# Spectral filter layer: 32 filter rows become 16, split by token parity over two halves of the rows, with summed and differenced output matrices

## Chip, cores and metric

The kernel runs on one core of a Trainium2 chip. The metric is the device time in microseconds (us) of one launch; before the change the median of three runs is 7736.49 us (7729.43 to 7759.1). The engines are named as the profile names them: PE is TensorE (PEld its weight loads), DVE is VectorE, ACT is ScalarE, POOL is GpSimd, SP is SyncE, whose queue issues nearly all DMAs here.

## What is computed

A network of four layers works on x of 64 images, each 11 x 11 = 121 tokens of 128 channels, in float32. Each layer adds a state-space mixer and then a feed-forward part to x. Only the feed-forward part of the last layer (index 3), a spectral transform unit, is changed. Cut to what matters:

```python
# phi: 16 filters in time; sgn(t) = +1 for even t, -1 for odd t
U_plus[t, k]  = sum_{s<=t} phi[k, t-s] * u[s]                    # per image and channel
U_minus[t, k] = sgn(t) * sum_{s<=t} phi[k, t-s] * sgn(s) * u[s]
out  = sum_k sigma[k]**0.25 * (U_plus[:, k] @ Mpp[k] + U_minus[:, k] @ Mpm[k])
out += sum_{i<3} shift(u, i) @ Mu[i]
# four such results for the first T, T//2, T//4, T//8 tokens, each with its own M,
# mixed by the weights softmax(log_weights + gumbel) in straight-through form
x = x + mix(layernorm(x))
```

The tokens fall into four bands: 0 to 14, 15 to 29, 30 to 59 and 60 to 120. A band gets contributions from as many of the four results as reach it; the last band has only the first.

## The kernel before, in words

Tokens lie on the partitions: `X` is a view of `HX`, 121 rows (D) by 64 images by 128 channels. The state-space mixer uses the same memory for its scan, and at its end loads X from DRAM in groups of eight images (L878, and L880 for the last group, which is stored last). After the feed-forward part, X is stored in groups of eight (L1432).

`stu_layer` (L1226) is emitted in program order, and a scheduler of the language then orders each engine's instructions by priority (program order) and readiness in its own model of time, so that a later instruction can go ahead of one that isn't ready. It handles the waits between engines. The parts are:

- Set-up. `stu_filters` forms the filters for the three early bands. `ahead` (L1254) holds the 16 filters as Toeplitz matrices; a matmul with the reversed identity `turned` (L1259) puts its rows in token order, and ScalarE copies the columns of the last band into `filt` (L1260). `filt` is scaled by sigma (L1266). A second set of 16 rows is made from the first with the signs of token and column (L1271), for U_minus. `M` (L1275), 32 matrices of 128 x 128, comes by one DMA; `MU` is the three shift matrices.
- `turned_in(b0)` (L1298) normalises eight images into `u`, and puts their transposes, with channels on the partitions, into `uT`.
- `last_band(b0, u)` (L1321) makes the last band for eight images. For each eight of the 32 filter rows, eight matmuls `pu` (L1327), one an image, have the image's tokens and channels as weights and 8 filters x 61 columns as moving data; VectorE and ScalarE copy the results in turn (`leave`, L1290) into `U`. Then eight matmuls `acc` (L1330) multiply `U` with the matrices and add up in one PSUM tile. Three more (L1332) add the shifts. The sum goes to `oT`.
- `matrices(i)` (L1308) folds a seventh of the filter matrices for the early bands: it loads a piece `m` (L1314), multiplies (L1316), copies to `ka` and stores it to `KD` in DRAM (L1319). The loop at L1348 goes over the first seven groups of images: `turned_in` of the next, `last_band` of this one, `matrices`.
- Then come the early bands in the order 2, 1, 0 (L1354): matmuls of all images against matrices read back from `KD` (L1370), summed in the PSUM tile `out` of four banks, which one buffer serves for all three bands; copies to `oT` (L1380).
- `turned_out` (L1337) transposes `oT` back, eight images at a time, and VectorE adds it to X. The last group's `last_band` and `turned_out` come at the very end.

PSUM has eight banks: three buffers for `mm` tiles (`pu`, `pt`, `pa`, `px`), one for `acc`, four for `out`. In the mixture-of-experts layer of layer 0, `moe_layer`, the matmul `px<-oe,P` (L1061) takes 64 rows of tokens' experts, at row 0 for one half and row 64 for the other.

Of the kernel before, what the change touches and what calls it, by code (L numbers as in the profile page):

```python
# [8 lines left out]
F32 = mybir.dt.float32  # L9
BF16 = mybir.dt.bfloat16  # L10
AF = mybir.ActivationFunctionType
ALU = mybir.AluOpType
AX = mybir.AxisListType
PSUM = bass.MemoryType.PSUM
DRAM = bass.MemoryType.DRAM

D = 121
C = 128
L = 256
NS = 16  # L20
E = 64
BANDS = ((0, 15), (15, 30), (30, 60), (60, 121))


class Ctx:
# [12 lines left out]
        nc.vector.memset(self.eps5, 1e-5)  # L38


def bcast(ap, n):

    return ap.unsqueeze(2).to_broadcast([ap.shape[0], ap.shape[1], n])


def layer_norm(cx, pool, dst, src, eps):

    nc = cx.nc
    G = src.shape[1]
    st = pool.tile([D, G, 6], F32, name="ln_st")  # L50
    mv = pool.tile([D, G, 2], F32, name="ln_mv")
    r = pool.tile([D, 2, G], F32, name="ln_r")
    for i in range(G):
        nc.vector.bn_stats(st[:, i, :], src[:, i, :])
    for i in range(G):
        nc.vector.bn_aggr(mv[:, i, :], st[:, i, :])

    nc.scalar.activation(r[:, 0, :], mv[:, :, 1], AF.Ln, bias=eps[:D])
    nc.scalar.activation(r[:, 0, :], r[:, 0, :], AF.Exp, scale=-0.5)
    nc.vector.scalar_tensor_tensor(r[:, 1, :], mv[:, :, 0], -1.0, r[:, 0, :], ALU.mult, ALU.mult)  # L60

    def apply():
        for i in range(G):
            nc.scalar.activation(
                dst[:, i, :], src[:, i, :], AF.Identity, bias=r[:, 1, i : i + 1], scale=r[:, 0, i : i + 1]
            )

    return apply
# [11 lines left out]
CB = 8  # L80
# [18 lines left out]
class Conv:  # L99
# [679 lines left out]
    def run(self):  # L779
        NC, G = self.NC, 2 * self.NC * PAIRS  # L780
# [92 lines left out]
        assert not self.plan and not early and not self.pre  # L873
        ahead()
        load(1)
        X = self.cx.X
        for c in range(NC - 1):
            self.nc.sync.dma_start(X[:, CB * c : CB * c + CB, :], self.dst(CB * c, CB))  # L878
        finish()
        self.nc.sync.dma_start(X[:, CB * NC - CB :, :], self.dst(CB * NC - CB, CB))  # L880


def conv_part(cx, v):
# [342 lines left out]
def stu_layer(cx, l, load):  # L1226
# [1 line left out]

    tc, nc, a, X, NB = cx.tc, cx.nc, cx.a, cx.X, cx.NB
    ident = cx.ident
    p = f"L{l}_ffn_"
    GB = 8
    CC = 2400
    T3 = BANDS[3][0]
    N3 = D - T3
    with ExitStack() as ctx:
        enter = ctx.enter_context
        keep = enter(tc.tile_pool(name=f"sk{l}", bufs=1))  # L1240
        work = enter(tc.tile_pool(name=f"sx{l}", bufs=2))
        ps = enter(tc.tile_pool(name=f"sp{l}", bufs=3, space=PSUM))
        ps_a = enter(tc.tile_pool(name=f"sa{l}", bufs=1, space=PSUM))

        sw = stu_filters(cx, l, keep)


        filt = keep.tile([D, 32, N3], F32, name="filt")
        phi = a[p + "phi"]
        nf, span = phi.shape  # L1250


        ahead = work.tile([D, 16, D], F32, name="ahead", tag="U")
        nc.sync.dma_start(ahead, bass.AP(tensor=phi.tensor, offset=phi.offset, ap=[[1, D], [span, nf], [1, D]]))  # L1254
        turned = keep.tile([D, D], F32, name="turned")
        nc.vector.tensor_copy(turned, ident[:D, D - 1 :: -1])
        for f in range(0, 16, 8):
            pf = ps.tile([D, 8, N3], F32, name="pf", tag="mm")
            nc.tensor.matmul(pf, turned, ahead[:, f : f + 8, T3:], start=True, stop=True)  # L1259
            nc.scalar.copy(filt[:, f : f + 8, :], pf)  # L1260
        sigma = keep.tile([D, 16], F32, name="sigma")
        nc.sync.dma_start(sigma, a[p + "sigma"].to_broadcast([D, 16]))
        nc.scalar.activation(sigma, sigma, AF.Sqrt)
        nc.scalar.activation(sigma, sigma, AF.Sqrt)
        nc.vector.tensor_scalar_mul(sigma, sigma, sw[:D, 0:1])
        nc.vector.tensor_mul(filt[:, 0:16, :], filt[:, 0:16, :], bcast(sigma, N3))  # L1266

        sgn = keep.tile([D, 2], F32, name="sgn")
        nc.sync.dma_start(sgn, a["sgn"])
        for odd in range(2):  # L1270
            nc.vector.tensor_scalar_mul(filt[:, 16:32, odd:N3:2], filt[:, 0:16, odd:N3:2], sgn[:, odd : odd + 1])  # L1271


        M = keep.tile([C, 32, C], F32, name="M")
        nc.sync.dma_start(M, a[p + "M"][:32].rearrange("k (d e) -> d k e", e=C))  # L1275
        MU = keep.tile([C, 4, 3, C], F32, name="MU")
        for i in range(4):
            z = 3 - i
# [5 lines left out]

        load()
        uT = keep.tile([C, NB, D], F32, name="uT")
        oT = keep.tile([C, NB, D], F32, name="oT")
        turn = 0

        def leave(dst, src):  # L1290
            nonlocal turn
            turn += 1
            if turn % 2:
                nc.vector.tensor_copy(dst, src)  # L1294
            else:
                nc.scalar.copy(dst, src)  # L1296

        def turned_in(b0):  # L1298
            u = work.tile([D, GB, C], F32, name="u", bufs=3)
            layer_norm(cx, work, u, X[:, b0 : b0 + GB, :], cx.eps5)()  # L1300
            for b in range(0, GB, 4):
                pt = ps.tile([C, 4, D], F32, name="pt", tag="mm")
                for i in range(4):
                    nc.tensor.transpose(pt[:, i, :], u[:, b + i, :], ident[:D, :D])
                leave(uT[:, b0 + b : b0 + b + 4, :], pt)
            return u

        def matrices(i):  # L1308

# [10 lines left out]

        def last_band(b0, u):  # L1321
            acc = ps_a.tile([C, GB, N3], F32, name="acc")
            for f0 in range(0, 32, 8):
                U = work.tile([C, 8, GB, N3], F32, name="U")
                for b in range(GB):
                    pu = ps.tile([C, 8, N3], F32, name="pu", tag="mm")
                    nc.tensor.matmul(pu, u[:, b, :], filt[:, f0 : f0 + 8, :], start=True, stop=True)  # L1327
                    leave(U[:, :, b, :], pu)
                for f in range(8):
                    nc.tensor.matmul(acc, M[:, f0 + f, :], U[:, f], start=(f0 + f == 0), stop=False)  # L1330
            for j in range(3):
                nc.tensor.matmul(  # L1332
                    acc, MU[:, 3, j, :], uT[:, b0 : b0 + GB, T3 - j : D - j], start=False, stop=(j == 2)
                )
            leave(oT[:, b0 : b0 + GB, T3:], acc)

        def turned_out(b0):  # L1337
            for b in range(b0, b0 + GB, 4):
                px = ps.tile([D, 4, C], F32, name="px", tag="mm")
                for i in range(4):  # L1340
                    nc.tensor.transpose(px[:, i, :], oT[:, b + i, :], ident)
                xs = X[:, b : b + 4, :]
                nc.vector.tensor_add(xs, xs, px)
# [10 lines left out]
        for z in (2, 1, 0):  # L1354
            t0, t1 = BANDS[z]
            n = t1 - t0
            per = min(512 // n, NB)
            out = ps_a.tile([C, 4, 512], F32, name="out")
            for k0 in range(0, NZ[z], KL):
                kn = min(KL, NZ[z] - k0)  # L1360
                K = work.tile([C, KL, C], F32, name="K", bufs=3)
                r0 = R0[z] + k0
                nc.sync.dma_start(K[:, :kn, :], cx.KD[r0 : r0 + kn].rearrange("r (d e) -> d r e", e=C))
                if k0 == 0:
                    nc.vector.tensor_add(K[:, :3, :], K[:, :3, :], MU[:, z])
                for k in range(k0, k0 + kn):
                    s0 = max(t0, k)
                    for i in range(-(-NB // per)):
                        b0, bn = i * per, min(per, NB - i * per)
                        nc.tensor.matmul(  # L1370
                            out[:, i, : bn * n].rearrange("p (b t) -> p b t", t=n)[:, :, s0 - t0 :],
                            K[:, k - k0, :],
                            uT[:, b0 : b0 + bn, s0 - k : t1 - k],
                            start=(k == 0),
                            stop=(k == NZ[z] - 1),
                            skip_group_check=True,
                        )
            for i in range(-(-NB // per)):
                b0, bn = i * per, min(per, NB - i * per)
                leave(oT[:, b0 : b0 + bn, t0:t1], out[:, i, : bn * n].rearrange("p (b t) -> p b t", t=n))  # L1380
        for b0 in range(0, end, GB):
            turned_out(b0)
        last_band(end, u)
# [7 lines left out]
def metaformer_kernel(ctx: ExitStack, tc: tile.TileContext, a: dict, out: bass.AP):  # L1391
# [32 lines left out]
    for l in range(4):  # L1424
        conv_part(cx, v)
        kept.close()
        if l < 3:
            v, kept, passing, weights = mixer(l + 1)
        dst = outr if l == 3 else mid[2 * l + 1]
        FFN[l](cx, l, weights if l < 3 else lambda: None)  # L1430
        for b0 in range(0, NB, GB):
            nc.sync.dma_start(dst[:, b0 : b0 + GB, :], cx.X[:, b0 : b0 + GB, :])  # L1432
        if l < 3:
            passing.close()

# [59 lines left out]
```

## Time and profile before

| What | us |
|---|---|
| median of three runs | 7736.49 |
| the profiled execution's own time | 7752.68 |
| its span, first to last instruction | 7750.9 |
| the chain leaves the mixer (last load of X issued) | 6962 |
| PE's first matmul of the changed layer (L1259) | 6992.8 |
| first `pu` / first `acc` matmul | 6999.0 / 7006.4 |
| one pass of the loop over groups of images | 65.2 to 66.8 |
| early bands (L1370) | 7464.4 to 7677.9 |
| last group's `last_band` | 7686.8 to 7743 |

The mean granted TensorE clock is 0.85 over the span, and 0.95 to 0.97 in the loop's passes. The busy time of all engines over the span: PE 6041.0, DVE 5659.8, ACT 5449.4, POOL 5293.3 us.

How to read the lines. A group of instructions is given by line, engine, operation, `out<-in` by the program's names, shapes (for PE: rows*columns of the weights, then partitions x elements of the moving data) and count, then busy time and mean ns of one, then the engine's idle time just before them and what ended it. A stretch (A:B) gives for each engine its busy time and, in brackets, the number of instructions, then the granted PE clock, the share of time the DMA engines were busy and GB/s. The chain of waits follows the work that ended last back in time: start, us, what. A float32 matmul appears as two records. Matmuls are pipelined and their ends are modelled, so their starts say more than their lengths.

### The profile page before, as it was taken

How to read it: one execution, taken by the hardware profiler on the slowest of the kernel's cores; microseconds unless marked ns; L12 is line 12 of the kernel's file. 1: busy time of each engine (PE TensorE's matmuls, PEld its weight loads, DVE VectorE, ACT ScalarE, POOL GpSimd, SP SyncE). 2: the span in 40 equal slices, each digit the busy share in tenths (PEclk: the TensorE clock that was granted, in tenths of full speed). 3: DMA queues.
4: the chain of work that ended last, by engine and by line, in shares of the span. 5: the costliest groups of instructions: out<-in, count | busy, mean ns of one | idle time of the engine just before them, and what ended most of it. 6: DMA issues, size and time to landing. Idle time of an engine off the chain costs nothing. (4 is left out here: it accounts for less than half of the span.)

```text
span 7750.9 us, 208787 instructions
## 1 busy us (share of the span) xinstructions
PE 6041.0 (78%) x84334; PEld 3448.5 (44%) x84334; DVE 5659.8 (73%) x7849; ACT 5449.4 (70%) x12343; POOL 5293.3 (68%) x2659
## 2 busy tenths in 40 slices
PE   6788778776788877766788888767678887758999
PEld 3444444465344444444344444434344444434445
DVE  5888888844788888962788888871788888872201
ACT  7888888733888888853788888862788888852200
POOL 6798999812888888931888888940888898960000
PEclk8888898777898989875889989875788888879999
DMA  7899999856899999942899999951899999971111
GB/s 181 227 247 243 245 246 243 215 167 170 221 241 249 246 240 244 247 110 75 220 241 244 246 248 243 243 140 37 217 236 243 243 245 241 245 184 46 35 39 36
DMA packets 905471, 1536.54 MB, mean 198 GB/s; under 512 B 136840, under 2 KB 617442, under 8 KB 904503
## 3 DMA queue, kind: packets, MB, share of 16 engines
q1 hardware_dynamic: 903223, 1521.09, 76.3%
q8 instruction: 662, 10.85, 0.6%
q14 instruction: 306, 2.51, 0.1%
q10 hardware_dynamic: 1280, 2.10, 0.1%
HBM read 1265.98 MB, written 256.97 MB: 196 GB/s over the span
## 5 line engine op out<-in xcount | busy, mean ns | idle before, releaser
L675 POOL TENSOR_TENSOR ub<-ub,Bt 128x1024 f32<-128x1024 f32 (+1 forms) x1984 | 4557.2, 2323 | 589.7 <-DMA ub<-uD 447.1
L699 ACT ACTIVATE da<-da,A 128x255 f32<-128x255 f32 x7744 | 3291.7, 451 | 696.1 <-PE da L686 612.0
L707 DVE TENSOR_TENSOR_SCAN H<-da,ub 128x512 f32<-128x512 f32 x2048 | 2391.8, 1208 | 354.4 <-POOL ub L675 183.9
L707 DVE TENSOR_TENSOR_SCAN HX<-da,ub 128x512 f32<-128x512 f32 (+1 forms) x1856 | 2130.4, 1190 | 318.5 <-POOL ub L675 160.1
L686 PE MATMUL da<-R,pick 120*128 120x255 bf16 x7744 | 1658.9, 305 | 546.0 <-DVE H L707 277.3
L686 PEld LDWEIGHTS <-pick 120*128 120x128 bf16 x7744 | 662.9, 103 | 1494.6 <-issue 1054.9
L728 PE MATMUL yb<-H,Cz 128*16 128x64 f32 x32768 | 782.2, 236 | 187.7 <-ACT yst L745 107.7
L728 PE MATMUL yb<-HX,Cz 128*16 128x64 f32 x32768 | 813.4, 237 | 122.6 <-DVE HX L707 62.7
L728 PEld LDWEIGHTS yb<-HX,Cz 128*16 128x16 f32 x32768 | 531.3, 105 | 641.9 <-issue 338.1
L728 PEld LDWEIGHTS yb<-H,Cz 128*16 128x16 f32 x32768 | 540.9, 103 | 584.0 <-issue 313.3
L263 PE MATMUL pc<-w_conv,xnT 128*121 128x256 f32 x1344 | 458.7, 433 | 27.4 <-ACT d L358 18.6
L184 POOL MEMSET t<- 128x2048 f32 x4 | 7.2, 1805 | 599.6 <-PE px L1221 211.8
L313 PE MATMUL pd<-t,w_dt 122*128 122x512 f32 x480 | 317.6, 749 | 101.7 <-ACT t L274 55.1
L745 ACT COPY yst<-yb 128x512 f32<-128x512 f32 (+2 forms) x640 | 334.9, 551 | 83.9 <-DMA yD<-yst 70.2
L743 DVE TENSOR_TENSOR yst<-yst,yb 128x512 f32<-128x512 f32 (+2 forms) x640 | 337.1, 543 | 73.7 <-PE yb L728 73.2
L340 PE MATMUL pr<-sp,ident 128*128 128x512 f32 x480 | 302.7, 717 | 80.0 <-ACT sp L301 75.0
L333 POOL TENSOR_TENSOR u<-sp,t 128x512 f32<-128x512 f32 x240 | 307.6, 1282 | 33.9 <-DMA uD<-u 32.8
L1294 DVE COPY U<-pu 128x488 f32<-128x488 f32 x128 | 85.4, 667 | 282.5 <-PE pu L1327 282.5
L1296 ACT COPY U<-pu 128x488 f32<-128x488 f32 x128 | 72.9, 570 | 308.7 <-PE pu L1327 308.7
L652 POOL TENSOR_TENSOR Cz<-Cp,own 128x512 f32<-128x512 f32 x256 | 275.5, 1076 | 0.0
L329 ACT CAST d<-sp 128x512 bf16<-128x512 f32 x240 | 148.6, 619 | 172.1 <-DMA dD<-d 171.9
L263 PEld LDWEIGHTS pc<-w_conv,xnT 128*121 128x121 f32 x1344 | 211.7, 194 | 94.9 <-ACT d L358 25.0
(237 smaller groups left out, 7243.8 us busy)
## 6 DMA issues: line engine op xcount, KB each, us to landing
ub<-uD SPq DMA_DIRECT2D x1920, 512.0 KB
dD<-d SPq DMA_DIRECT2D x256, 384.0 KB
R<-dD SPq DMA_DIRECT2D x192, 420.0 KB
uD<-u SPq DMA_DIRECT2D x256, 256.0 KB
yD<-yst SPq DMA_DIRECT2D x512, 60.5 KB
y<-yD SPq DMA_DIRECT2D x112, 242.0 KB
bcD<-bc SPq DMA_DIRECT2D x128, 128.0 KB
w1g<-in_L_ffn_weight_dram SPq DMA_DIRECT2D x16, 1024.0 KB
```

The costliest lines, as they stand in the source:

```text
L263: nc.tensor.matmul(pc, lhs, rhs, start=(j == 0), stop=(j == taps - 1))
L313: nc.tensor.matmul(s["p"], self.w_dt[:, k, :], tb[: D + 1], start=True, stop=True)
L333: nc.gpsimd.tensor_mul(s["u"], s["sp"], tb)
L340: nc.tensor.matmul(s["pr"], self.cx.ident, s["sp"], start=True, stop=False, skip_group_check=True)
L652: self.nc.gpsimd.tensor_mul(self.Cz[u], C.unsqueeze(2).to_broadcast([128, 64, CB]), self.own.unsqueeze(1).to_broadcast([128, 64, CB]),)
L675: self.nc.gpsimd.tensor_mul(x, x, self.bc[m, "Bt"].unsqueeze(1).to_broadcast([128, n, L]))
L686: self.nc.tensor.matmul(self.da[g % RING][:, j, 1:], self.pick[:n, d % 5].rearrange("p n b -> p (n b)"), self.R[m, d // 35][:n, d % 35 // ...
L699: self.nc.scalar.activation(x, x, AF.Exp, scale=self.A[:, m % 2, d : d + 1])
L707: self.nc.vector.tensor_tensor_scan(self.H[dq % 2][:, :n, p - DQ[dq][0]], self.da[g % RING].rearrange("p j l -> p (j l)")[:, :n], x.rearra ...
L728: self.nc.tensor.matmul(self.yb[32 * q : 32 * q + 16, slot % 8, :, :, :w], self.Cz[slot // 8][:, place % 64 : place % 64 + 2, :].rearrange ...
L743: nc.vector.tensor_add(dst, dst, src)
L745: nc.scalar.copy(dst, src)
```

## The change

In `stu_layer`, X, `u` and `filt` are laid out by token parity: even tokens in rows 0 to 60, odd tokens in rows 64 to 123 (`ROWS` is 124). With E and O the sums over even and odd tokens, U_plus is E + O, and U_minus is E - O at even output tokens and O - E at odd ones. So `pu` makes E and O with the same 16 filter rows, from the two halves of the rows, in matmuls of 61 or 60 rows and 4 filters x 61 columns, alternately on either half, and with two images to a PSUM tile. The matrices become Mpp + Mpm and Mpp - Mpm: E at even tokens and O at odd ones take the sum, the others the difference. `acc` is split by output parity into 31 and 30 columns for eight images. The columns of `filt` have even tokens first. The same `oT` gets its columns by parity, so that transposing it gives X's new rows. X is loaded and stored with one DMA for each parity in layer 3; layers 0 to 2 keep theirs. `mm` tiles get seven buffers, and `out` becomes tiles of that kind, one bank each; `U` becomes two tiles of 4 filters with four buffers in all; `ahead` takes a buffer of `u`.

```diff
+    def parted(self, b, n):
+        for rows, odd in ((slice(0, ODD - 3), 0), (slice(ODD, ROWS), 1)):
+            yield self.HX[rows, b * C : (b + n) * C].rearrange("p (b c) -> p b c", c=C), odd
+
+    def load_x(self, l, b, n, src):
...
+        for x, odd in self.parted(b, n):
+            self.nc.sync.dma_start(x, src[odd::2])
...
-        ps = enter(tc.tile_pool(name=f"sp{l}", bufs=3, space=PSUM))
+        ps = enter(tc.tile_pool(name=f"sp{l}", bufs=7, space=PSUM))
...
-        ahead = work.tile([D, 16, D], F32, name="ahead", tag="U")
+        ahead = work.tile([D, 16, D], F32, name="ahead", tag="u", bufs=3)
...
-        for odd in range(2):
-            nc.vector.tensor_scalar_mul(filt[:, 16:32, odd:N3:2], filt[:, 0:16, odd:N3:2], sgn[:, odd : odd + 1])
...
+        for k in range(0, 16, 8):
+            low = work.tile([C, 8, C], F32, name="low", tag="U", bufs=4)
+            nc.vector.tensor_sub(low, M[:, 0, k : k + 8], M[:, 1, k : k + 8])
+            nc.vector.tensor_add(M[:, 0, k : k + 8], M[:, 0, k : k + 8], M[:, 1, k : k + 8])
+            nc.scalar.copy(M[:, 1, k : k + 8], low)
...
+            pt = [ps.tile([C, GB, ODD - 3], F32, name="pt", tag="mm") for _ in range(2)]
+            for i in range(GB):
+                for odd, rows in enumerate((slice(0, ODD - 3), slice(ODD, ROWS))):
+                    n = rows.stop - rows.start
+                    nc.tensor.transpose(pt[odd][:, i, :n], u[rows, i, :], ident[rows, rows])
...
-            for f0 in range(0, 32, 8):
-                U = work.tile([C, 8, GB, N3], F32, name="U")
-                for b in range(GB):
-                    pu = ps.tile([C, 8, N3], F32, name="pu", tag="mm")
-                    nc.tensor.matmul(pu, u[:, b, :], filt[:, f0 : f0 + 8, :], start=True, stop=True)
-                    leave(U[:, :, b, :], pu)
-                for f in range(8):
-                    nc.tensor.matmul(acc, M[:, f0 + f, :], U[:, f], start=(f0 + f == 0), stop=False)
+            for f0 in range(0, 16, 4):
+                U = [work.tile([C, 4, GB, N3], F32, name="U", bufs=4) for _ in range(2)]
+                for b in range(0, GB, 2):
+                    pu = [ps.tile([C, 2, 4, N3], F32, name="pu", tag="mm") for _ in range(2)]
+                    for i in range(2):
+                        for s in range(2):
+                            rows = slice(ODD, ROWS) if s else slice(0, ODD - 3)
+                            nc.tensor.matmul(
+                                pu[s][:, i], u[rows, b + i, :], filt[rows, f0 : f0 + 4, :], start=True, stop=True
+                            )
+                    for s in range(2):
+                        leave(U[s][:, :, b : b + 2, :].rearrange("c f b t -> c b f t"), pu[s])
+                for f in range(4):
+                    for m in range(2):
+                        for odd, c0, c1 in halves:
+                            nc.tensor.matmul(
+                                acc[:, :, c0:c1],
+                                M[:, m, f0 + f, :],
+                                U[m ^ odd][:, f, :, c0:c1],
...
+            out_by_rows(b0, GB, T3, acc, True)
...
-            out = ps_a.tile([C, 4, 512], F32, name="out")
+            out = [ps.tile([C, 512], F32, name="out", tag="mm") for _ in range(-(-NB // per))]
```

More of the change, by code (lines that the diff above doesn't have):

```diff
@@ L22 @@
 BANDS = ((0, 15), (15, 30), (30, 60), (60, 121))
+ODD = 64
+ROWS = ODD + D // 2
 class Ctx:
@@ L38, in __init__, with store_x @@
         nc.vector.memset(self.eps5, 1e-5)
+    def parted(self, b, n):
+        for rows, odd in ((slice(0, ODD - 3), 0), (slice(ODD, ROWS), 1)):
+            yield self.HX[rows, b * C : (b + n) * C].rearrange("p (b c) -> p b c", c=C), odd
+    def load_x(self, l, b, n, src):
+        if l < 3:
+            self.nc.sync.dma_start(self.X[:, b : b + n, :], src)
+            return
+        for x, odd in self.parted(b, n):
+            self.nc.sync.dma_start(x, src[odd::2])
+    def store_x(self, l, b, n, dst):
+        if l < 3:
+            self.nc.sync.dma_start(dst, self.X[:, b : b + n, :])
+            return
+        for x, odd in self.parted(b, n):
+            self.nc.sync.dma_start(dst[odd::2], x)
 def bcast(ap, n):
@@ L49, in layer_norm @@
     G = src.shape[1]
-    st = pool.tile([D, G, 6], F32, name="ln_st")
-    mv = pool.tile([D, G, 2], F32, name="ln_mv")
-    r = pool.tile([D, 2, G], F32, name="ln_r")
+    n = src.shape[0]
+    st = pool.tile([n, G, 6], F32, name="ln_st")
+    mv = pool.tile([n, G, 2], F32, name="ln_mv")
+    r = pool.tile([n, 2, G], F32, name="ln_r")
     for i in range(G):
@@ L56, in layer_norm @@
         nc.vector.bn_aggr(mv[:, i, :], st[:, i, :])
-    nc.scalar.activation(r[:, 0, :], mv[:, :, 1], AF.Ln, bias=eps[:D])
+    nc.scalar.activation(r[:, 0, :], mv[:, :, 1], AF.Ln, bias=eps[:n])
     nc.scalar.activation(r[:, 0, :], r[:, 0, :], AF.Exp, scale=-0.5)
@@ L875, in run @@
         load(1)
-        X = self.cx.X
         for c in range(NC - 1):
-            self.nc.sync.dma_start(X[:, CB * c : CB * c + CB, :], self.dst(CB * c, CB))
+            self.cx.load_x(self.l, CB * c, CB, self.dst(CB * c, CB))
         finish()
-        self.nc.sync.dma_start(X[:, CB * NC - CB :, :], self.dst(CB * NC - CB, CB))
+        self.cx.load_x(self.l, CB * NC - CB, CB, self.dst(CB * NC - CB, CB))
 def conv_part(cx, v):
@@ L1226, in stu_layer @@
 def stu_layer(cx, l, load):
-    tc, nc, a, X, NB = cx.tc, cx.nc, cx.a, cx.X, cx.NB
+    tc, nc, a, NB = cx.tc, cx.nc, cx.a, cx.NB
+    X = cx.HX[:ROWS].rearrange("p (b c) -> p b c", c=C)
     ident = cx.ident
@@ L1237, in stu_layer @@
     N3 = D - T3
+    NE = N3 - N3 // 2
+    halves = ((0, 0, NE), (1, NE, N3))
     with ExitStack() as ctx:
@@ L1241, in stu_layer @@
         work = enter(tc.tile_pool(name=f"sx{l}", bufs=2))
-        ps = enter(tc.tile_pool(name=f"sp{l}", bufs=3, space=PSUM))
+        ps = enter(tc.tile_pool(name=f"sp{l}", bufs=7, space=PSUM))
         ps_a = enter(tc.tile_pool(name=f"sa{l}", bufs=1, space=PSUM))
         sw = stu_filters(cx, l, keep)
-        filt = keep.tile([D, 32, N3], F32, name="filt")
+        filt = keep.tile([ROWS, 16, N3], F32, name="filt")
         phi = a[p + "phi"]
         nf, span = phi.shape
-        ahead = work.tile([D, 16, D], F32, name="ahead", tag="U")
+        ahead = work.tile([D, 16, D], F32, name="ahead", tag="u", bufs=3)
@@ L1254, in stu_layer @@
         nc.sync.dma_start(ahead, bass.AP(tensor=phi.tensor, offset=phi.offset, ap=[[1, D], [span, nf], [1, D]]))
-        turned = keep.tile([D, D], F32, name="turned")
-        nc.vector.tensor_copy(turned, ident[:D, D - 1 :: -1])
+        turned = keep.tile([D, ROWS], F32, name="turned")
+        nc.vector.memset(turned, 0.0)
+        nc.vector.tensor_copy(turned[:, : ODD - 3], ident[:D, D - 1 :: -2])
+        nc.vector.tensor_copy(turned[:, ODD:], ident[:D, D - 2 : 0 : -2])
         for f in range(0, 16, 8):
-            pf = ps.tile([D, 8, N3], F32, name="pf", tag="mm")
-            nc.tensor.matmul(pf, turned, ahead[:, f : f + 8, T3:], start=True, stop=True)
-            nc.scalar.copy(filt[:, f : f + 8, :], pf)
@@ L1261, in stu_layer @@
-        sigma = keep.tile([D, 16], F32, name="sigma")
-        nc.sync.dma_start(sigma, a[p + "sigma"].to_broadcast([D, 16]))
+            for odd, c0, c1 in halves:
+                pf = ps.tile([ROWS, 8, NE], F32, name="pf", tag="mm")
+                pf = pf[:, :, : c1 - c0]
+                nc.tensor.matmul(pf, turned, ahead[:, f : f + 8, T3 + odd :: 2], start=True, stop=True)
+                nc.scalar.copy(filt[:, f : f + 8, c0:c1], pf)
+        sigma = keep.tile([ROWS, 16], F32, name="sigma")
@@ L1263, in stu_layer @@
+        nc.sync.dma_start(sigma, a[p + "sigma"].to_broadcast([ROWS, 16]))
         nc.scalar.activation(sigma, sigma, AF.Sqrt)
         nc.scalar.activation(sigma, sigma, AF.Sqrt)
[L1265 to L1269, printed above, removed]
-        for odd in range(2):
-            nc.vector.tensor_scalar_mul(filt[:, 16:32, odd:N3:2], filt[:, 0:16, odd:N3:2], sgn[:, odd : odd + 1])
@@ L1274, in stu_layer @@
-        M = keep.tile([C, 32, C], F32, name="M")
-        nc.sync.dma_start(M, a[p + "M"][:32].rearrange("k (d e) -> d k e", e=C))
+        nc.vector.tensor_scalar_mul(sigma, sigma, sw[:ROWS, 0:1])
+        nc.vector.tensor_mul(filt, filt, bcast(sigma, N3))
+        M = keep.tile([C, 2, 16, C], F32, name="M")
+        nc.sync.dma_start(M.rearrange("d s k e -> d (s k) e"), a[p + "M"][:32].rearrange("k (d e) -> d k e", e=C))
+        for k in range(0, 16, 8):
[3 more added lines that the diff above has]
+            nc.scalar.copy(M[:, 1, k : k + 8], low)
@@ L1286, in stu_layer @@
         uT = keep.tile([C, NB, D], F32, name="uT")
-        oT = keep.tile([C, NB, D], F32, name="oT")
+        oT = keep.tile([C, NB, ROWS], F32, name="oT")
+        nc.gpsimd.memset(oT[:, :, ODD - 3 : ODD], 0.0)
         turn = 0
@@ L1298, in turned_in, with out_by_rows @@
         def turned_in(b0):
-            u = work.tile([D, GB, C], F32, name="u", bufs=3)
+            u = work.tile([ROWS, GB, C], F32, name="u", bufs=3)
             layer_norm(cx, work, u, X[:, b0 : b0 + GB, :], cx.eps5)()
[L1301 to L1305, printed above, removed]
-            return u
+            pt = [ps.tile([C, GB, ODD - 3], F32, name="pt", tag="mm") for _ in range(2)]
[3 more added lines that the diff above has]
+                    nc.tensor.transpose(pt[odd][:, i, :n], u[rows, i, :], ident[rows, rows])
+            for odd in range(2):
+                leave(uT[:, b0 : b0 + GB, odd::2], pt[odd][:, :, : ODD - 3 - odd])
+            return u
+        def out_by_rows(b0, n, t0, src, parted):
+            for odd in range(2):
+                first = t0 + (t0 + odd) % 2
+                rows = len(range(first, t0 + src.shape[2], 2))
+                r0 = ODD * odd + first // 2
+                part = src[:, :, NE * odd : NE * odd + rows] if parted else src[:, :, first - t0 :: 2]
+                leave(oT[:, b0 : b0 + n, r0 : r0 + rows], part)
         def matrices(i):
@@ L1331, in last_band @@
-            for j in range(3):
[L1332 to L1335, printed above, removed]
+            for f0 in range(0, 16, 4):
[12 more added lines that the diff above has]
+                    for m in range(2):
+                        for odd, c0, c1 in halves:
+                            nc.tensor.matmul(
+                                acc[:, :, c0:c1],
+                                M[:, m, f0 + f, :],
+                                U[m ^ odd][:, f, :, c0:c1],
+                                start=(f0 + f == 0 and m == 0 and odd == 0),
+                                stop=False,
+                                skip_group_check=True,
+                            )
@@ L1337, in turned_out @@
+            for j in range(3):
+                for odd, c0, c1 in halves:
+                    nc.tensor.matmul(
+                        acc[:, :, c0:c1],
+                        MU[:, 3, j, :],
+                        uT[:, b0 : b0 + GB, T3 + odd - j : D - j : 2],
+                        start=False,
+                        stop=(j == 2),
+                        skip_group_check=True,
+                    )
+            out_by_rows(b0, GB, T3, acc, True)
         def turned_out(b0):
             for b in range(b0, b0 + GB, 4):
-                px = ps.tile([D, 4, C], F32, name="px", tag="mm")
+                px = ps.tile([ROWS, 4, C], F32, name="px", tag="mm")
@@ L1370, in stu_layer @@
                         nc.tensor.matmul(
-                            out[:, i, : bn * n].rearrange("p (b t) -> p b t", t=n)[:, :, s0 - t0 :],
+                            out[i][:, : bn * n].rearrange("p (b t) -> p b t", t=n)[:, :, s0 - t0 :],
                             K[:, k - k0, :],
@@ L1379, in stu_layer @@
                 b0, bn = i * per, min(per, NB - i * per)
-                leave(oT[:, b0 : b0 + bn, t0:t1], out[:, i, : bn * n].rearrange("p (b t) -> p b t", t=n))
+                out_by_rows(b0, bn, t0, out[i][:, : bn * n].rearrange("p (b t) -> p b t", t=n), False)
         for b0 in range(0, end, GB):
@@ L1431, in metaformer_kernel @@
         for b0 in range(0, NB, GB):
-            nc.sync.dma_start(dst[:, b0 : b0 + GB, :], cx.X[:, b0 : b0 + GB, :])
+            cx.store_x(l, b0, GB, dst[:, b0 : b0 + GB, :])
         if l < 3:
```

## Prediction

> **What bounds the kernel now.** I read the page first: VectorE, ScalarE and GpSimd carry the span up to about slice 36 and fade in the last ones, where the changed layer runs. Then the chain of waits from 7059.9 to 7126 us, one pass of the loop over batch groups:
>
> ```profile
> by line: PE acc L1330 40.3%; PE pu L1327 39.9%; DMA m<-in_L_ffn_M_dram 9.6%; PE pa L1316 6.3%; PE acc L1332 3.7%; PE pt L1304 2.4%; ACT ka L1296 0.9%; SPq L1319 0.5%; issue 0.4%; SPq L1314 0.0%
> ...
> 7064.75 7.56 PE pu L1327 x18
> 7072.31 6.66 PE acc L1330 x16
> 7078.97 6.55 PE pu L1327 x16
> 7085.52 6.66 PE acc L1330 x16
> ...
> 7122.71 0.57 ACT ka L1296
> ...
> 7123.30 0.34 SPq L1319
> ...
> 7123.75 3.07 DMA m<-in_L_ffn_M_dram
> ```
>
> PE is the path. `pu` (tokens against filters) and `acc` (filters against matrices) take four bursts each, 26 us apiece per call of `last_band`; there are eight calls, 420 us. Every float32 matmul is two records (x16 for eight), called passes here: 6.55/16 = 0.409 us for 488 columns, or 0.84 ns a column. The other end: 4.24 us per loop pass (7122.71 to 7126.95) in which PE waits for one piece of the matrices.
>
> **Can two halves of the rows run at once?** The mixture-of-experts layer already has matmuls on row halves (L1061, 64 rows at row 0 or 64). Rows by shape over the whole span, and two stretches of all engines:
>
> ```profile
> L1061 PE MATMUL px<-oe,P 64*121 64x128 f32 x128 | 17.3, 401 | 14.5 <-DVE oe L1051 14.5
> ...
> L1061 PEld LDWEIGHTS px<-oe,P 64*121 64x121 f32 x128 | 16.7, 288 | 15.3 <-DVE oe L1051 9.7 <-issue 5.5
> ```
> ```profile
> 1818.70:1820.70 2.00, 2.00 (x29) 1.95 (x27) 2.00 (x4) 0.00 (x0) 0.00 (x0) 0.99 0.69 178
> 7079.00:7085.00 6.00, 6.00 (x16) 2.66 (x15) 2.00 (x3) 1.97 (x4) 0.00 (x0) 1.00 0.00 0
> ```
>
> A 128-column pass streams for 128 x 0.84 = 107 ns. In 1818.70 to 1820.70, at clock 0.99, 29 passes started in 2.00 us, 69 ns each: 1.55 at a time, changes of group included. Record by record, one half starts passes at 1819.278, .387 and .496, the other at .382, .491 and .600: each half keeps its own 109 ns while the other runs. So halves do overlap, in float32, at full clock.
>
> **The gain.** `pu` before: 64 passes x 0.409 = 26.2 us a call. After: 16 filters x 61 columns x 8 batches on two halves is 64 matmuls, 128 passes, of 244 columns, 0.206 us, two abreast: 64 x 0.206 = 13.2. Gain 13.0 a call, 104 us in eight.
>
> Weights: 128 passes need 128 loads. The row: L1061 loads 121 columns for each pass and still keeps 109 ns, so the load lies behind the stream of the same half. Against it stands the Trainium skill, "TensorE: Matmul & The Clock Gate", Part 3, The mechanism: a weight load overlaps with running matmuls only when its row group differs. By that rule each half would take 0.107 + 0.206 = 0.313 a pass, `pu` 20.0 us a call, and the gain would be 6.2 a call, 50 us. I take the row, since it is the same machine, type and tiling; the rule stays as a rival.
>
> **Costs.**
> - Changes between row halves and the full array. None of that very pair is in the trace; nearest is full array to the 16-column form (weight loads on PE's load queue, then matmuls):
>
> ```profile
> 883.51 0.51 PEld L525 LDWEIGHTS po<-out_wT,g 128*121 128x121 f32 x4
> 884.15 0.35 PEld L728 LDWEIGHTS yb<-HX,Cz 128*16 128x16 f32 x24
> ```
> ```profile
> 883.62 0.60 PE L525 MATMUL po<-out_wT,g 128*121 128x128 f32 x4
> 884.15 0.53 PE L728 MATMUL yb<-HX,Cz 128*16 128x64 f32 x24
> ```
>
> Four passes at 0.109 from 883.62 end at 884.06; L728's load comes at 884.15, 0.09 later, whereas L525's load at 883.51 went ahead of its turn. A change costs 0.09 plus the load it keeps from going ahead (0.105 in a first `acc` pass, 677 against 572 ns). About 9 a call x 0.195, less the 4 x 0.105 already paid: 1.3 a call, 10 us. Ends: 0 and 20.
> - `acc` keeps its columns (32 pairs of filter and matrix set x 488) but as 128 passes of 248 or 240, in runs of 31 and 30. Runs cost little: L1332, in eight runs of 61, has 0.413 against 0.409 (1%); L1370, in runs of 30 or shorter, took 153.34 us for 87,360 x 2 columns that stream in 145.6 (5%). I take 3%: 0.8 a call, 6 us; ends 2 and 11. Loads of 0.107 fit behind 0.2. L1332 becomes 12 passes of half length that read every second element; no row shows that, ends nothing and double (2.5 a call, 20 us), I take 0.5 us in all.
> - Emptying `pu`: as many copies of 488 elements as before (667 ns on VectorE, 570 on ScalarE), but a pair every 0.82 us instead of one. The skill's "TensorEngine Tiling (Array Packing)", PSUM Bottleneck, warns that copies may become the limit: 0.67 with a start of some 0.06 fits in 0.82, so not in the stream. At each burst's end the last copy ends about 0.9 us after the last pass; before, the next burst's first matmul (0.82) filled this (x18). Filled, it costs 0; not at all, 0.9 x 32 = 29 us. The seven PSUM buffers allow filling: a third, 10 us.
> - The start. M is folded by four VectorE operations of 128x1024 (1.22 us each at L1051) and two copies. M is in before 7000.66, where MU behind it in the queue is used, so the first `acc`, at 7006.4 before, could start near 7005, with two bursts of `pu` ahead of it. VectorE also has `filt`, `uT` and MU to do; queued behind a fold that waits for M they hold PE up. 4 us, ends 0 and 8.
> - DMAs: each X load and store becomes two on SP, 0.4 us more each. Seven of eight loads are issued from 6942.47 to 6946.4 and SP is free until 6956.36; without that cover they would cost 2.8. The last one delays what stands behind it on SP, `ahead` among it, by 0.4; PE waits for that load (35.4 us). The last store adds 0.3. The sign load that goes stood behind `ahead`, so frees nothing. Sum 0.7.
> - `ahead` moves into the three buffers of `u`, so only two groups can be normalised ahead of the first `pu` instead of three. Their work lies in PE's 35.4 us wait; the third is first needed two loop passes later, so nothing is lost.
> - Layer norm on 124 rows, folding filters by parity (same columns) and twice as many half transposes (two abreast) come to about nothing; within 3 us.
> - Bands z = 2, 1, 0 get PSUM tiles of their own, so the next band no longer waits for the last one's copies: 2.66 + 1.36 us go (idle before `out`, "ACT oT"). Next is the K load, issued 12 us ahead. Copies by parity, twice as many, lie beside PE except before the last transposes (0.3): 3.7 gained; ends 0 and 4.
>
> What is late next is still PE: in the loop pass of 65.87 us from 7059.98 VectorE is busy for 13.49 us and ScalarE for 17.41, and neither gets more than the copies above.
>
> Sum: 104 - 10 - 6 - 0.5 - 10 - 4 - 0.7 + 3.7 = 76 us. The profiled execution is 7752.68 (span 7750.9 and 1.8 around it), 16 above the median of 7736.49. The saving is taken at the median: 7661.
>
> The 4.24 us wait for `m` comes seven times, 30 us. SP issues loads in order behind stores of `ka`; shorter bursts give those transfers less cover, a changed order of PE could give more. I leave it; gone it would make 7631, doubled 7691.
>
> **Rivals.**
> 1. As worked out, waits moving by some 25 us either way: 7636 to 7695. 0.66.
> 2. Burst ends are filled and the wait for `m` shrinks: 76 + 10 + up to 30, 7620 to 7636. 0.12. For it: seven buffers; against: only SP's order could do it, and that is unchanged.
> 3. Weight loads not hidden (the rule): 76 - 54 = 22, so 7715. 0.10. Against it the 109 ns.
> 4. The halves don't overlap, loads hidden: `pu` stays at 26.4, the change doesn't do what it says; 10 + 6 + 4 are paid: 7755. 0.06. Semaphores between short passes could do this; L1061 has eight passes to a wait, this four.
> 5. Slower: the halves don't overlap and loads aren't hidden. `pu` is 128 x 0.313 = 40.1, +13.9 a call, 111, with the 17 of the other costs 7864. It begins where the mean spacing of `pu` passes exceeds 0.18 us, since (26.2 - 3.3)/128 = 0.18 is what is left after the costs. Against it 69 ns for half the columns. 0.06.
>
> **The numbers.** This kernel's measurement can't tell less than 0.5% (39 us) from no change. Under 7698: cases 1 and 2, 0.78. Within: cases 3 and 4, 0.16. Slower: case 5, 0.06. From 7620 to 7716 leaves out cases 4 and 5 and little below.
>
> **What would show it.** `pu`: 128 passes a call, bursts near 3.3 us instead of 6.55, means near 370 ns (a 238-column pass of L1370 shows 369), spacing near 0.103. Bursts of 5.0 say case 3, of 6.6 case 4. `acc` bursts of 6.8. First `acc` after a burst: idle on U copies at most 0.3 us. Loop pass near 55 us instead of 65.5. Wrong if `pu`'s spacing is over 0.13, if a change costs over 0.4 us, or if the wait for `m` grows past 8 us.

## The result and the profile after

The changed kernel takes 7768.77 us (median of 13 runs, 7756.4 to 7784.41) against 7747.19 us for the kernel before (median of 13 runs, among them the three above): 1.0029 times as long, 95% interval 1.0022 to 1.0037. The forecast was 7661, and 7620 to 7716 as the range, so 0.9902 of its base of 7736.49. The medians of the kernel before differ by some 20 us between the chips and occasions of these runs, so from here on only ratios to the kernel before in the same set of runs are compared.

The new arithmetic works. The chain of waits in one pass of the loop over groups of images, in the changed kernel (start, us, what; `pu` is now L1369, `acc` L1377):

```profile
7157.43 4.47 PE pu L1369 x32
7161.90 0.66 DVE U L1323
7162.56 0.04 issue
7162.60 6.92 PE acc L1377 x32
7169.52 3.11 PE pu L1369 x28
7172.63 0.02 issue
7172.65 0.68 DVE U L1323
7173.33 0.04 issue
7173.37 6.92 PE acc L1377 x32
...
7202.20 2.69 PE acc L1387 x12
...
7206.75 3.85 DMA m<-in_L_ffn_M_dram
```

From one `acc` burst to the next it is 10.77 us (7162.60 to 7173.37), where the prediction's lines have 13.21 (7072.31 to 7085.52). A `pu` burst of 32 passes takes 3.11 us for the 28 in the chain and the time of four more; it was 6.55. `acc` grows from 6.66 to 6.92. A loop pass takes 55.3 to 56.1 us (the mean of two passes in a row, since they alternate) instead of 65.2 to 66.8. The time is lost at both ends of the layer. SP's queue just before it, in the kernel before and then in the changed one, where seven groups of X are loaded:

```profile
6942.47 3.89 SPq L878 DMA_DIRECT2D HX<-mid  x7
6956.36 0.28 SPq L618 DMA_DIRECT2D mid<-xo  x1
```
```profile
6921.15 54.67 SPq L52 DMA_DIRECT2D HX<-mid  x14
6975.93 6.97 SPq L640 DMA_DIRECT2D mid<-xo  x1
```

Seven loads took SP 3.89 us to issue; fourteen take it 54.67, far more than twice. The mixer's last two stores wait behind them (`mid<-xo`), and with these the last load and all of the layer's set-up. The same at the end, in the DMA view of the changed kernel from 7707 to 7755 us (40 slices: the busy share of 16 engines in tenths, then GB/s):

```profile
DMA  0000044000000003600000000170000000007100
GB/s 22 22 22 22 22 120 114 22 22 22 22 22 22 22 22 87 147 22 21 22 22 22 22 22 22 51 184 22 22 22 22 22 22 22 22 27 200 29 11 0
```

PE is done at 7707; for 47 us the last stores run on, at 22 GB/s most of the time and at 114 to 200 in short bursts between: every second DMA is slow. The 16 stores of half groups are issued from 7654.17 on and hold SP for 95.47 us, some 12 us a pair.

The mixer ahead of this layer ends anywhere from 6936 to 6988 us in these profiles, whatever the kernel, so the layer is measured from the end of the last mixer's last matmul (the matmuls `po<-out_wT,H`). The segments, worked out from starts in the traces, in us:

| Segment | before | changed | split_60_1 (below) |
|---|---|---|---|
| mixer's last matmul to the layer's first (`pf`) | 35.3 | 99.4 | 35.6 |
| to the first `acc` | 13.6 | 16.9 | 17.2 |
| to the first early-band matmul | 458.0 | 390.4 | 390.5 |
| early bands | 213.5 | 208.7 | 208.5 |
| to the last transpose (last group) | 67.1 | 55.7 | 55.6 |
| to the end | 5.9 | 47.4 | 5.7 |
| sum | 793.4 | 818.5 | 713.1 |

So the changed layer gains 80.5 us in its four middle segments and loses 64.1 + 41.5 = 105.6 at the ends. The balance, 25 us, agrees with the 22 us (0.29% of 7747) of the runs.

### The profile page after: what moved, and what is told of

Same layout as the page of the kernel before. It is cut to its first block, busy times and chain, and to the rows that moved or that the text cites. A ratio compares the mean times of both kernels' runs of the same rounds, so it can differ in the third digit from the quotient of the medians.

```text
span 7754.5 us, 211095 instructions
## 1 busy us (share of the span) xinstructions
PE 5969.8 (77%) x85474; PEld 3559.4 (46%) x85474; DVE 5666.1 (73%) x7861; ACT 5474.7 (71%) x12359; POOL 5293.0 (68%) x2660
## 4 chain that ended last, share of the span: by engine, by line
PE 22%; ACT 13%; DMA 11%; DVE 9%; issue 7%; POOL 4%; SPq 1%; DVEq 0%; ACTq 0%; POOLq 0%
ACT da L721 7%; DMA dD<-d 4%; DMA ub<-uD 3%; DVE H L729 3%; PE yb L750 3%; PE acc L1377 3%; POOL ub L697 3%; PE out L1430 3%; PE da L708 2%; PE pc L285 2%; DVE HX L729 2%; PE pst L1235 2%; PE pu L1369 1%; PE po L547 1%; DMA yD<-yst 1%
## 5 line engine op out<-in xcount | busy, mean ns | idle before, releaser
L335 PE MATMUL pd<-t,w_dt 122*128 122x512 f32 x480 | 315.9, 745 | 105.0 <-ACT t L296 55.7
L1377 PE MATMUL acc<-U,M 128*128 128x248 f32 (+1 forms) x1024 | 222.3, 373 | 7.4 <-DVE U L1323 4.1
```

Of the source, the lines that this page charges most:

```text
L335: nc.tensor.matmul(s["p"], self.w_dt[:, k, :], tb[: D + 1], start=True, stop=True)
L1377: nc.tensor.matmul(acc[:, :, c0:c1], M[:, m, f0 + f, :], U[m ^ odd][:, f, :, c0:c1], start=(f0 + f == 0 and m == 0 and odd == 0), stop=Fal ...
```

## The experiments

**What makes the loads and stores slow.** Three things are new in them: 61 rows (even tokens) and 60 (odd tokens) in place of 121; a step of two rows in DRAM; and twice as many. The first theory says that a DMA of 61 rows runs on one of the 16 DMA engines. The Trainium skill, "DMA: Bandwidth & Descriptors", Why a DMA increments its semaphore by 16 and not by 1, states the rule: a DMA uses the largest number of engines up to 16 that divides the slowest dimension of both sides. That makes 11 for 121 rows, 15 for 60, and 1 for 61, a prime. The traces agree: the next to last figure of a stretch is the share of the 16 engines that were busy. First the tail of the changed kernel, where only a 61-row store runs; then, with transfers crowding the queue, the loads of 121 rows in the kernel before, and those of 60 rows (split_60_1, below); last a stretch of a 58-row store (before_58_63, below), for which the rule gives 2:

```profile
7716.00:7720.00 4.00, 0.00 (x0) 0.00 (x0) 0.00 (x0) 0.00 (x0) 0.00 (x0) 0.50 0.07 22
6950.00:6952.00 2.00, 0.00 (x0) 0.00 (x0) 0.00 (x0) 2.00 (x7) 1.05 (x1) 0.50 0.70 240
6980.00:6982.00 2.00, 0.00 (x0) 0.00 (x0) 0.00 (x0) 2.00 (x6) 0.97 (x2) 0.50 0.97 229
7752.00:7753.00 1.00, 1.00 (x3) 0.38 (x2) 0.00 (x0) 0.00 (x0) 0.00 (x0) 1.00 0.14 43
```

The shares are 0.07, 0.70, 0.97 and 0.14, where 1, 11, 15 and 2 engines of 16 would be 0.06, 0.69, 0.94 and 0.13. The loads of 60 rows, on 15 engines, get no more than those of 121 rows on 11 (229 against 240 GB/s); one engine gets a tenth of that. What the 61 rows cost the kernel is tested by four kernels, compared with the kernel before on one chip. The first cuts the 61 rows:

```diff
+    def parted3(self, b, n):
+        for r0, r1, odd in ((0, 60, 0), (60, 61, 120), (ODD, ROWS, 1)):
+            at = slice(odd, odd + 2 * (r1 - r0) - 1, 2)
+            yield self.HX[r0:r1, b * C : (b + n) * C].rearrange("p (b c) -> p b c", c=C), at
...
-        for x, odd in self.parted(b, n):
-            self.nc.sync.dma_start(x, src[odd::2])
+        for x, at in self.parted3(b, n):
+            self.nc.sync.dma_start(x, src[at])
```

> The changed kernel with each 61-row DMA of even tokens (load and store of X in layer 3) cut into 60 rows and 1 row; nothing else. Theory A (a DMA of 61 rows runs on one of the 16 engines, since 61 has no divisor to share it by; some 24 GB/s): PE's first matmul of the layer comes back from 7035 to about 6994 and the tail after the last transposes shrinks from 47 us to 6 to 8, so 80 us less than the changed kernel, about 7685 us against 7747 of the kernel before. Theory B (it is the step of two rows in DRAM): no change, 7765 to 7770. Theory C (it is the number of DMAs on SP): 16 more DMAs, 5 to 10 us slower than the changed kernel.

Measured: 0.9898 of before (0.9881 to 0.9915), 79 us less at 7766 (66 to 92 by the interval), and 1.3% or some 102 us less than the changed kernel (0.9898/1.0029), where 80 were expected. It has 24 loads and 24 stores, more than the changed kernel's 16 of each, so their number is not the cause. SP's queue in its profile:

```profile
6972.61 13.84 SPq L57 DMA_DIRECT2D HX<-mid  x21
6986.56 2.98 SPq L645 DMA_DIRECT2D mid<-xo  x2
```

21 loads hold SP for 13.84 us, and the table's last column shows both ends back at the values of before. The second and third kernel take the other way round, and put the cut alone into the kernel before:

```diff
-            self.nc.sync.dma_start(X[:, CB * c : CB * c + CB, :], self.dst(CB * c, CB))
+            for r in parts(self.l):
+                self.nc.sync.dma_start(X[r, CB * c : CB * c + CB, :], self.dst(CB * c, CB)[r])
```

In layer 3 the parts are rows 0 to 60 and 61 to 120 in the one, and in the other 60 even rows, row 120 and 60 odd rows; the last load and the stores are cut alike.

> The kernel before with each load and store of X in layer 3 as two DMAs, of rows 0 to 60 and 61 to 120, without any step of two rows and with nothing of the new computation. Theory A (61 rows go to one DMA engine): about 80 us slower, 7825. Theory B (step of two rows): within 2 us of before. Theory C (number of DMAs): 1 to 5 us slower.

> The kernel before with each load and store of X in layer 3 as three DMAs: even rows 0 to 118 (60 rows, step of two), row 120 alone, odd rows 1 to 119 (60 rows, step of two). Theory A (61 rows go to one DMA engine): 1 to 5 us slower than before. Theory B (step of two rows): about 80 us slower. Theory C (number of DMAs): as A or a little more.

Measured: the plain cut into 61 and 60 costs 1.0111 (1.0096 to 1.0126), 86 us, with nothing of the new computation and no step in DRAM. The step of two with 60 rows costs nothing: 0.9994 (0.9985 to 1.0003). Only the first theory fits both. In the chain of before_61_60 the loads appear as in the changed kernel, about 10 us for each pair:

```profile
6954.61 9.76 SPq L883
6964.41 0.91 SPq L883
6965.37 8.99 SPq L883
6974.41 1.07 SPq L883
6975.52 9.90 SPq L883
...
7007.01 15.23 DMA mid<-xo
7022.59 12.48 DMA HX<-mid
```

The two last lines show the rest of the harm: the mixer's store takes 15.23 us from issue to landing, and the last load of X, itself of 61 rows, 12.48, where the layer waits for it. The store keeps its 121 rows. In the changed kernel, where it takes 15.22 us (from 6983.02), the engines' share is 0.07 at 27 GB/s from 6990 to 6994: one engine is still at work on what is in the queue. In split_60_1 the store takes 3.22. So the 64.1 us of the changed kernel's start are, by its chain and that of split_60_1, some 46 us by which the store is issued late, 12 by which it lands late, and 6 after that, for the last load and the set-up.

The fourth kernel cuts only the stores of the changed kernel:

> The changed kernel with only the stores cut into 60, 60 and 1 rows; the loads keep 61 and 60. Theory A: the tail goes (about 40 us less than the changed kernel, 7727), PE's first matmul of the layer stays at about 7035. Theory B: no change. Theory C: some 3 us slower than the changed kernel.

Measured: 0.9977 (0.9968 to 0.9987), 0.52% or 40 us less than the changed kernel. The remaining 0.79% to split_60_1, 61 us, is the loads' share. Both agree with the table's 41.5 and 64.1, and so does this kernel's profile: 100.4 us from the mixer's last matmul to `pf`, 5.9 from the last transpose to the end.

**Is it the divisor, or any uneven count?** The kernel before once more, cut at row 58. The largest divisors up to 16 are 2 for 58 rows and 9 for 63:

```diff
-    return (slice(0, 61), slice(61, 121)) if l == 3 else (slice(0, D),)
+    return (slice(0, 58), slice(58, 121)) if l == 3 else (slice(0, D),)
```

> The kernel before with each load and store of X in layer 3 as two DMAs, of rows 0 to 57 and 58 to 120. Theory A (a DMA uses as many of the 16 engines as the largest divisor of its rows up to 16: 58 gives 2, 63 gives 9, where 61 gives 1): a 58-row DMA takes about 5 us instead of 10, the loads hold SP some 20 us too long, the last store costs 3 more, so 20 to 28 us slower than before. Theory B (every count that doesn't divide by 16, or every odd cut, goes to one engine): as before_61_60, some 93 us slower. Theory C (only primes are slow): within 5 us of before.

Measured: 1.0032 (1.0018 to 1.0046), 25 us, as theory A says and neither of the others. SP's queue for the seven groups:

```profile
6955.54 28.83 SPq L883 DMA_DIRECT2D HX<-mid  x14
```

28.83 us instead of 54.94 in before_61_60: two engines (0.14 above), about half the time.

**Does the gain hang on alternating the halves?** The forecast rested on two halves that run abreast, read from a place where runs of eight passes follow one another. This kernel is split_60_1 with the passes of a burst in another order:

```diff
-                for b in range(0, GB, 2):
-                    pu = [ps.tile([C, 2, 4, N3], F32, name="pu", tag="mm") for _ in range(2)]
-                    for i in range(2):
-                        for s in range(2):
+                for s in range(2):
+                    for b in range(0, GB, 2):
+                        pu = ps.tile([C, 2, 4, N3], F32, name="pu", tag="mm")
+                        for i in range(2):
```

> split_60_1 with only the order of the pu matmuls changed: within a burst of four filters all 16 passes of the even half of the rows come first, then all 16 of the odd half, same matmuls, copies and sums. Theory A (PE looks only a few passes ahead, as at L1061, where a half started with three passes of the other still to come; the gain needs the halves in alternation): bursts grow from 3.4 us to about 5.9, 32 bursts, so some 80 us slower than split_60_1, about 7775. Theory B (the look-ahead spans a whole half burst, 32 loads and passes): the halves still run abreast, bursts stay near 3.4 us, 7690 to 7700.

Measured: 1.0041 of before (1.0017 to 1.0064), 1.4% or 111 us slower than split_60_1, and 118 us by the segments of the layer (831.3 against 713.1); the gain is gone. PE in one burst and around it:

```profile
7098.73 5.73 PE L1374 MATMUL pu<-filt,u 61*128 61x244 f32 x30
7104.38 0.69 PE L1381 MATMUL acc<-U,M 128*128 128x248 f32 x2
7105.01 0.68 PE L1374 MATMUL pu<-filt,u 61*128 61x244 f32 x2
7105.61 6.50 PE L1381 MATMUL acc<-U,M 128*128 128x240 f32 x30
```

Bursts are 5.66 us in the chain, near the 5.9 expected. In the trace's records the odd half's first pass starts at 7100.897, after the even half's 7100.891, when three more of the even half are to come (7101.097, .303, .509), all of which stand before it in the program. At L1061 in the kernel before it is the same: a half starts at 1819.174 with three passes of the other to come (1819.278, .387, .496). So PE looks ahead by about four passes in both places, and only those run abreast.

The loss is larger than the 80 us expected. From one `acc` burst to the next it is 13.31 us instead of 10.74, 2.6 more; that is some 70 us for 27 of the 32 bursts. The other five follow a wait for `m` and take 11.66 us, wholly at half clock, instead of 4.1 to 5.2, and the passes behind them are slow too: the granted clock is still 0.50 from 7149 to 7156, 22 us after the wait ended at 7134.47. In split_60_1, where such a wait ends at 7143.24, it is 1.00 again from 7148.1. Why the low clock lasts longer here was not tried.

**What is the wait for `m` worth?** It was left standing in the forecast at 30 us. Split_60_1 with six buffers for each of two tiles:

```diff
-                m = work.tile([128, CC // 5], F32, name="m")
+                m = work.tile([128, CC // 5], F32, name="m", bufs=6)
...
-                ka = work.tile([R0[3], CC // 5], F32, name="ka")
+                ka = work.tile([R0[3], CC // 5], F32, name="ka", bufs=6)
```

> split_60_1 with six buffers instead of two for the pieces m and ka of matrices(), nothing else. Theory A (PE's wait for m, 4.3 us in each of seven loop passes, comes from two buffers: the third load can't be issued before a piece is multiplied): the wait goes, 25 to 30 us less than split_60_1, about 7667 against 7766 of before. Theory B (it comes from the order on SP's queue, where loads stand behind stores of ka that wait for PE): no change, 7690 to 7700.

Measured: 0.9843 of before (0.9825 to 0.9862), 122 us less; it is the fastest of all. Against split_60_1 it gains 0.56%, 43 us, but the two intervals leave some 20 us on either side. The segments of the layer are sharper: from the first `acc` to the early bands it takes 354.1 us instead of 390.5, 36 us less. The seven waits come to 29 us at most in the chain of split_60_1, so at least 7 us of the gain are not the waits themselves. The chain of one loop pass shows why:

```profile
7166.31 3.22 PE pa L1360 x8
7169.53 0.64 PE pt L1339 x13
7170.17 3.41 PE pu L1374 x29
```

In four of the six loop passes of split_60_1 that begin with such a wait, the transposes take 1.04 us and the first burst 4.1 to 5.2; here they take 0.64 and 3.41, as in the other two. The granted PE clock in two stretches of the loop, here in split_60_1 and below it in split_more_m (us, then busy time and count of PE, PEld, DVE, ACT, POOL, then the clock, DMA share and GB/s):

```profile
7090.00:7240.00 150.00, 141.07 (x829) 114.24 (x828) 38.36 (x60) 44.61 (x82) 0.00 (x0) 0.95 0.12 36
7240.00:7360.00 120.00, 111.60 (x632) 89.74 (x632) 27.52 (x43) 30.11 (x59) 0.00 (x0) 0.97 0.14 42
```
```profile
7090.00:7240.00 150.00, 147.22 (x881) 120.83 (x880) 40.17 (x63) 50.12 (x94) 0.00 (x0) 1.00 0.15 46
7240.00:7360.00 120.00, 117.83 (x707) 97.14 (x707) 32.77 (x50) 30.60 (x57) 0.00 (x0) 1.00 0.12 36
```

Without the waits the clock stays at 1.00; with them it drops to 0.50 for some us around most of them (0.50 from 7142 to 7147.5 in split_60_1). Not every wait of 4 us costs this: after the one that ended at 7256.53 the clock was 1.00. The two buffer counts were raised together; which of them was needed was not tried.

## Why the prediction was wrong, point by point

**The step that failed** is the one on DMAs: "each X load and store becomes two on SP, 0.4 us more each", with the sum 0.7 us. It priced a DMA by its issue on the queue alone and put what the transfer of 61 rows takes at nothing, without a reason. The measured cost is 105.6 us: 64.1 at the start, 41.5 at the end. The cover that it named, SP free from 6946.4 to 6956.36, was overrun many times over: the loads held SP for 54.67 us. The tail is a backlog. The stores hold SP for 95.47 us from 7654 on, and the last group's computation covers only 53 of them. None of the five rivals had this mechanism, and none of the listed signs of being wrong came true: passes of `pu` are 0.103 us apart on average, a change costs 0.2 and the wait for `m` stays under 5. The total alone would have misled: 22 us slower is close to what case 4 forecast (19), in which the halves don't overlap, and they do. The step could have been seen to fail beforehand: the new row counts stand in the diff, and the page cited above states the rule.

**Without that step the sum holds.** It gave 76 us; split_60_1, which differs from the changed kernel only in those DMAs, gains 79 us in the runs and 80.3 in the layer's segments. That it comes so close is in part luck, since single terms are off by up to 4 us in both directions. Term by term:

- `pu`, 104 us: right. In a burst each half starts a pass every 0.206 us, both at once (split_60_1: 7102.117, .323, .529 on the odd half; 7102.124, .330, .536 on the even one). Weight loads stay hidden, one of 128 columns behind each pass of the same half, as the row had it, against the rule of the Trainium skill's "TensorE: Matmul & The Clock Gate", Part 3, The mechanism, which the prediction kept as a rival: that a load overlaps only with another row group. The measurement decides.
- Changes between halves and full array, 0.09 + 0.105: right, in split_60_1. After the last `acc` pass at 7101.514 (240 columns, 0.200) the first load comes at 7101.806, 0.092 after the stream's end, and the next pass of the half 0.310 after its first instead of 0.206. The price of a change to the 16-column form carried over to row halves.
- Ends of bursts, 10 us: about right. From the start of the last `pu` pass to the first of `acc` it is 0.61 to 0.72 us; less the pass itself (0.206) and the 0.09, that leaves 0.3 to 0.4 a burst of waiting for the last copies, 10 to 13 us in all.
- `acc` in shorter runs: about right. Passes of 248 columns start 0.213 us apart and those of 240 columns 0.202, 0.208 on average, where 0.211 was taken. The chain's 6.92 for 32 holds the load of the change, counted above, and some 0.07 before the third pass, which waits for the second `U`. The every-second-element passes (L1387) take 2.69 us a call, up from 2.48, so reading that way costs at most 0.2 us a call.
- The start, 4 us: too low. The first `acc` comes 17.2 us after `pf` instead of 13.6, although its `pu` burst is shorter by 3.3, so about 7 are lost. In the chain of split_60_1 the fold (`low`, `M`) and then a copy into `U`, all on VectorE, follow the landing of M; PE stands still for 3.6 us before that copy, and from 7036 to 7042 its clock is 0.50.
- Early bands, 3.7: 4.8 to 5.0 gained.
- The wait for `m`: nearly unchanged, 4.3 to 4.9 us in six of the seven, as left; worth 36 us by the segments (43 by the runs) rather than 30, for the clock's sake.

## What to carry to other kernels

When an edit changes how many rows a DMA moves, work out how many engines the new count can use before costing it: a cut from 121 rows to 61 and 60 left half of the transfers with about a tenth of the bandwidth (22 to 27 GB/s against 229 to 240), and splitting off one row gave that back. Row halves of PE run abreast in float32 with their weight loads hidden, but only where the program alternates between them every few passes. A wait on PE of 4 us or more can cost more than its length, since work after it may run at half clock: here seven waits of 29 us at most were worth 36.

## What the runs showed that was not expected

- 61 rows: 22 GB/s for the stores, 26 to 27 for the loads of X; 58 rows halve the time on SP, and 60 rows with a step of two in DRAM cost nothing.
- A slow DMA harms what stands behind it on the queue more than its own reader: seven slow loads that nobody waited for yet delayed the issue of the mixer's last store by some 46 us, and all the set-up behind it.
- PE starts passes on one row half while earlier passes of the other are still to start, about four passes ahead; in a run of 16 on each half this leaves half of the array idle most of the time.
- Taking away seven waits, 29 us in all at most, gained 36 us.
- With the halves in turn the granted clock stayed at 0.50 for 22 us after a wait, and with the halves abreast for 5.
